# A graph layer on one core: the last steps in another order, and gathers without added waits on VectorE

## The chip, the cores and the metric

The kernel runs on one core of a Trainium2 chip. The metric is device time in microseconds (us), the median of several executions. TensorE (PE) multiplies matrices, and PEld is its loading of weights; VectorE (DVE) and ScalarE (ACT) work on elements; GpSimd (POOL) issues the indirect transfers (gathers) here; SyncE (SP) issues the plain ones, ACT a few of them.

## The reference

One message-passing layer, with residual and normalization. There are 12500 nodes with 128 features (`x`), and 400000 edges with source, destination (sorted) and length (`edge_weight`). What is computed, shortened:

```python
rbf = exp(-(d[:, None] - centers) ** 2 / (2 * width * width))      # 50 centers, 0 to 10
cut = 0.5 * (cos(pi * d / 10) + 1) * (d <= 10)
W = (silu(rbf @ fw1 + fb1) @ fw2 + fb2) * cut[:, None]
messages = (h[src] @ pw + pb) * W
agg = segment_sum(messages, dst)
y = x + (h + silu(agg @ mw1 + mb1) @ mw2 + mb2)                    # h is x
out = (y - mean(y)) / sqrt(var(y) + 1e-5)
```

Edges longer than 10 have `cut` 0 and give nothing.

## The kernel before, in words

Edges of length over 10 are dropped on the chip: in seven chunks (`pack`, `unpack`, L704 to L981) the kept edges are packed together, and they come out as 139 **quads** (`NL`) of 4 times 128 edges. `proj`, which is x times `pw` plus `pb`, is stored in HBM at the start; the first 12 quads gather rows of x and multiply them on the core.

The main loop (L1574) takes one quad `q` per step:

- `fetch` (L1082) gathers 128 rows per instruction (L1088), four to a quad, into one of 21 buffers (`quad`, `x`; 9 from quad 63 on); quads in `SINGLY`, 133 and 134 among them, have only three gathers and get their other rows by single transfers from SP or ACT. How far ahead gathers are put into POOL's queue is set by a planned clock (`clock`, `pool`) and by free buffers (`room`). For quads under `UPTO` (90) each gather has an added wait (L1091 to L1094): on the VectorE instruction that stands a number of places before it in program order, 66 to 19 by `BACK`.
- `basis(o)` (L1129): on ACT, square and exponential of the distances for two quads at once (L1140, L1144); `first(o)` (L1151) and `silu(o)` (L1159) make the hidden layer for them, on PE and ACT. `octs(q)` gives the pair `o` of a step, so that `basis`, `first` and `silu` come two steps or more ahead.
- `second(q + 2)` (L1167) multiplies by `fw2` on PE into a bank of PSUM. There are four such banks; they go round in one list (`bank`, `free`) with all other users.
- `message(q)` (L1178): one product on DVE, bank times gathered rows (L1189), which waits for the last gather of the quad. It gives the bank back.
- `place(q + 1)` (L1196): four instructions on DVE make the 128-wide one-hot tile `hot` (L1201), with `cut` in it. `sum_up(q)` (L1213) multiplies it with the messages on PE (L1221); `add(q)` (L1251) adds the sums into `aggT` on DVE (L1255).
- Nodes go in blocks `t0` of four tiles of 128 nodes, of two tiles from 88 on, as soon as their sums are complete: `node_first` (L1260: PE, then a silu on ACT, `zs`, L1270, which gives the bank back), `node_second` (L1274, PE), `node_stats` (L1299: DVE, L1305 and L1309), and for a group of blocks `variances`, `roots` and `scales` (L1311 to L1340: DVE, a square root on ACT at L1325, DVE). `normalize` (L1342) scales by tiles, on ACT (L1356) or DVE (L1353), and `store` issues the block's transfer to HBM. Blocks 0 to 76 (`early`) have their steps from `begin` (L1392 to L1401); their statistics come in groups of four blocks. 76 has its statistics in step 131.

Every engine works through its instructions in the order of the program; the text above is that order (`manual_schedule`). The last seven steps, quads 132 to 138, are written out one after the other (L1647 to L1753), with the blocks 76 to 96 between them. `house(q)` (L1627) does in them what the loop does for gathers. `keep_busy(n)` (L1435) issues n matmuls whose results nobody reads. The table of ACT's functions is reloaded (ACT_TABLE_LOAD) between square root, exponential and silu. In the step of quad 138 its four products are taken one by one, in `message(q, (0, 1))` and so on.

## Time and profile before

| | |
|---|---|
| runs shown, median of 3 | 720.64 us (720.64 to 723.32) |
| the profiled execution's own time | 718.53 us |
| its span, first to last instruction | 717.0 us |
| mean granted TensorE clock | 0.918 of full |
| DMA | 91.41 MB, mean 127 GB/s |

A profile row of an engine or line gives busy time and count; a row of the timeline gives start and duration in us from the start of the span, engine, line, operation, the program's names (out<-in), shapes, count, and in brackets the engine's idle time just before it and what ended that. Durations are of this one execution, so sums are made against its 718.53 us.

### The profile page before, as it was taken

What the parts mean: (1) busy time and instruction counts of PE and PEld (TensorE: products, weight loads), DVE (VectorE), ACT (ScalarE), POOL (GpSimd) and SP (SyncE); (2) the same over time, 40 slices, a digit from 0 to 9 for tenths busy, and PEclk for the clock granted to TensorE, in tenths of its full rate; (3) what the DMA queues carried; (4) which work ended last, traced back from release to release, by engine and by line L of the source; (5) the groups of instructions that cost most, each with busy time, mean ns of one, the idle gap of its engine ahead of it and who ended that gap; (6) DMA issues with size and microseconds to landing.
All of it is one profiled execution on the core that took longest, in us unless ns stands there. A gap on an engine that the chain in (4) does not pass through costs nothing.

```text
span 717.0 us, 14503 instructions
## 1 busy us (share of the span) xinstructions
PE 584.6 (82%) x3526; PEld 461.1 (64%) x3526; DVE 561.7 (78%) x1741; ACT 401.7 (56%) x569; POOL 529.2 (74%) x565
## 2 busy tenths in 40 slices
PE   5878868688898788697878997799998887878775
PEld 5767557566676576575666765577686654665554
DVE  8899899759998799989979994876856545555765
ACT  6557625245645667554645566466765843574564
POOL 6777777777777777777777777777777777777771
PEclk9998787899999899889987999699999998999997
DMA  8996533333334333443344334444543444344242
GB/s 259 328 328 206 161 99 102 98 102 84 115 103 130 83 87 100 118 126 85 87 113 118 99 116 116 130 131 120 153 113 91 138 111 114 101 142 126 56 131 79
DMA packets 54004, 91.41 MB, mean 127 GB/s; under 512 B 14272, under 2 KB 21536, under 8 KB 53914
## 3 DMA queue, kind: packets, MB, share of 16 engines
q0 software_dynamic: 17712, 36.51, 20.4%
q1 hardware_dynamic: 24916, 35.61, 15.0%
q10 hardware_dynamic: 11286, 18.31, 8.0%
q8 instruction: 29, 0.48, 0.3%
q14 instruction: 61, 0.50, 0.2%
HBM read 74.59 MB, written 15.79 MB: 126 GB/s over the span
## 4 chain that ended last, share of the span: by engine, by line
POOL 18%; DVE 15%; DMA 13%; issue 13%; PE 9%; ACT 3%; ACTq 3%; DVEq 1%; SPq 0%; POOLq 0%
POOL quad L1088 14%; DMA quad<-proj,srci 8%; POOL x L1088 3%; DVE hot L1201 3%; PE ph L1156 3%; DMA x<-proj,srci 3%; DVE msg L1189 2%; ACTq L1064 2%; PE sums L1221 2%; PE bank L1174 1%; DVE aggT L1255 1%; DMA packed<-line,at_i 1%; DVE quad L1189 1%; DMA pair<-packed 1%; DVE quad L1201 1%
## 5 line engine op out<-in xcount | busy, mean ns | idle before, releaser
L1088 POOL DMA_INDIRECT quad<-proj,srci x402 | 381.7, 950 | 122.6 <-issue 97.3
L1174 PEld LDWEIGHTS bank<-fw_sb,s 128*128 128x128 f32 x1112 | 158.1, 205 | 60.3 <-issue 50.2
L1174 PE MATMUL bank<-fw_sb,s 128*128 128x128 f32 x1112 | 158.2, 289 | 0.0
L1156 PE MATMUL ph<-rbf,w_sb 102*128 102x512 f32 x278 | 143.7, 642 | 12.3 <-ACT s L1162 8.3
L1221 PEld LDWEIGHTS sums<-hot,msg 128*128 128x128 f32 x816 | 109.2, 200 | 53.4 <-issue 26.0
L1162 ACT ACTIVATE s<-ph 128x1024 f32<-128x1024 f32 x70 | 71.2, 1017 | 122.3 <-PE ph L1156 121.9
L1201 DVE TENSOR_SCALAR hot<-iota_n,dl,cut 128x80 f32<-128x80 f32 (+4 forms) x408 | 111.1, 347 | 22.9 <-PE sums L1221 20.9
L1221 PE MATMUL sums<-hot,msg 128*128 128x80 f32 (+4 forms) x816 | 111.5, 282 | 15.4 <-DVE msg L1189 15.2
L1088 POOL DMA_INDIRECT x<-proj,srci x94 | 90.0, 958 | 28.7 <-issue 22.3
L1171 PE MATMUL bank<-fb_b,ones_b 96*128 96x512 bf16 x139 | 56.0, 403 | 42.2 <-DVE msg L1189 22.0
L1189 DVE TENSOR_TENSOR msg<-bank,quad 128x512 f32<-128x512 f32 (+1 forms) x78 | 52.5, 673 | 41.1 <-DMA quad<-proj,srci 34.5
L1156 PEld LDWEIGHTS ph<-rbf,w_sb 102*128 102x128 f32 x278 | 51.2, 205 | 51.7 <-issue 37.3
L1255 DVE TENSOR_TENSOR aggT<-aggT,sums 128x80 f32 (+4 forms) x209 | 54.1, 259 | 30.7 <-PE sums L1221 12.4
L1140 ACT ACTIVATE rbf<-d_sb,rbf_bias,rbf_scale 102x512 f32<-102x512 f32 x70 | 56.2, 803 | 8.0 <-issue 8.0
L1088 POOL DMA_INDIRECT quad<-in_x_dram,srci x48 | 47.5, 990 | 15.9 <-issue 12.5
L1162 ACT ACT_TABLE_LOAD x34 | 43.6, 1283 | 15.3 <-issue 14.9
L1144 ACT ACT_TABLE_LOAD x35 | 44.9, 1283 | 11.4 <-issue 9.6
L1221 PE MATMUL sums<-quad,quad 128*128 128x128 f32 (+3 forms) x296 | 41.8, 285 | 11.0 <-DVE quad L1189 11.0
L350 PEld LDWEIGHTS bank<-pw_sb,xT 128*128 128x128 f32 (+1 forms) x292 | 42.3, 209 | 11.2 <-issue 5.6
L1144 ACT ACTIVATE rbf<-rbf 102x512 f32<-102x512 f32 x70 | 44.1, 630 | 7.9 <-issue 5.6
L1221 PEld LDWEIGHTS sums<-quad,quad 128*128 128x128 f32 x296 | 38.6, 201 | 12.7 <-DVE quad L1189 12.4
L350 PE MATMUL bank<-pw_sb,xT 128*128 128x128 f32 (+1 forms) x292 | 42.8, 293 | 0.8 <-ACT xT L995 0.6
(281 smaller groups left out, 796.9 us busy)
## 6 DMA issues: line engine op xcount, KB each, us to landing
d_sb<-near_d ACTq DMA_DIRECT2D x67, 256.0 KB
row_sb<-proj SPq DMA_DIRECT2D x1024, 0.5 KB
x<-in_x_dram SPq DMA_DIRECT2D x46, 256.0 KB
row_sb<-proj ACTq DMA_DIRECT2D x512, 0.5 KB
quad<-proj,srci POOLq DMA_INDIRECT x402
proj<-hp SPq DMA_DIRECT2D x24, 256.0 KB
out_dram<-x SPq DMA_DIRECT2D x22, 256.0 KB
x<-proj,srci POOLq DMA_INDIRECT x94
```

Source lines behind the costliest of these rows:

```text
L350: nc.tensor.matmul(to[:m, k, :], lT[:, k * P:k * P + m], w, start=False, stop=(k == a + c - 1))
L1088: g = nc.gpsimd.indirect_dma_start(out=got[:, j, :], out_offset=None, in_=proj if table is None else table, in_offset=bass.IndirectOffsetO ...
L1140: a = nc.scalar.activation(rbf[:u], d[:u], AF.Square, bias=rbf_bias[:u], scale=rbf_scale[:u])
L1144: nc.scalar.activation(rbf[:u], rbf[:u], AF.Exp, scale=-1.0 / (2.0 * width * width))
L1156: nc.tensor.matmul(ph[:, h, :], w1_sb[:2 * KR, h, :], rbf[:2 * KR], start=True, stop=True)
L1162: nc.scalar.activation(s[:, :n], ph[:, :n], AF.Silu)
L1171: nc.tensor.matmul(pu, ones_b[:, :P], bias_b["fb2"].rearrange("k j f -> k (j f)"), start=True, stop=False)
L1174: nc.tensor.matmul(pu[:, j * H:(j + 1) * H], s[:, j * P:(j + 1) * P], fw2_sb, start=False, stop=(j == QT - 1))
L1189: nc.vector.tensor_mul(msg[:, a:b, :], pu_of[q].rearrange("p (j f) -> p j f", j=QT)[:, a:b, :], got_of[q][:, a:b, :])
L1201: nc.vector.tensor_scalar(hot[:, j, :wide(q)], iota_n[:, :wide(q)], dl[:, at[0], at[1]], cut[:, at[0], at[1]], op0=OP.is_equal, op1=OP.mult)
L1221: nc.tensor.matmul(pa[:, k * W:k * W + wide(q)], msg[:, j, :], hot[:, j, :wide(q)], start=(j % n == 0), stop=(j % n == n - 1))
L1255: nc.vector.tensor_add(to, to, pa[:, k * W:k * W + wide(q)])
```

## The change

Two things are changed.

*Gathers.* `BACK`, `UPTO`, `VECTORS`, the record of VectorE instructions and `behind` go, and with them the added wait in `fetch`. The waits that follow from the data (buffers free, indices there) stay.

*The last steps.*

- The bases of pairs 68 and 69, issued in step 131 so far, are issued in step 132 behind `place(133)`; `first` and `silu` of 68 and 69 go from steps 132 and 133 to 133 and 134.
- In the last steps `second(q + 2)` stands between `message(q)` and `sum_up(q)`, where it stood behind both.
- Block 76 leaves the last group of four: 64, 68 and 72 have their root in step 129 and are normalized in 130 to 132; 76 has its statistics at the end of step 130 and is in one group with 80, 84, 88 and 90.
- `node_stats` of 80 to 92 stand ahead of `add` or earlier; 76 and 80 are normalized together in step 136; block 88 is normalized on DVE; `node_x(96)` stands ahead of the sums of 136.
- `keep_busy` is called with 3, 2 and 2 in place of 1 and 1.

```diff
-            g = nc.gpsimd.indirect_dma_start(
+            nc.gpsimd.indirect_dma_start(
                 out=got[:, j, :], out_offset=None, in_=proj if table is None else table,
                 in_offset=bass.IndirectOffsetOnAxis(ap=i, axis=0))
-            if 0 <= q < UPTO and len(vectors) > behind(q):
-                tc.add_manual_dep(
-                    g.ins, vectors[-1 - behind(q)],
-                    mybir.DependencyInfo(mybir.DependencyClass.Sync, mybir.DependencyReason.DATA))
...
-            if begin[t0][2] == q:
+            if begin[t0][2] == q and t0 != early[-1]:
                 if k % 4 == 0:
                     st_of[0] = statistics()
                 node_stats(t0, st_of[0][:, k % 4 * 4:])
-                if k % 4 == 3:
+                if k % 4 == 3 or t0 == early[-2]:
                     deep.append(deviations(early[k // 4 * 4:k + 1], st_of[0]))
...
     def tail(q):
 
+        if q == NL - 9:
+            last_st.append(statistics())
+            node_stats(early[-1], last_st[0])
...
-                if 2 * o < NL:
+                if 2 * o < NL and q < NL - 8:
                     basis(o)
...
     q = NL - 7
     house(q)
-    sum_up(q, message(q))
+    msg = message(q)
     second(q + 2)
+    sum_up(q, msg)
+    node_second(84)
+    node_stats(80, last_st[:, 4:])
     bases_of(list(range(q, NL)))
     place(q + 1)
-    scales(*deep.pop(0))
+    for o in (octs(q), octs(q + 1)):
+        basis(o)
     add(q)
-    first(octs(q))
-    silu(octs(q))
-    node_second(84)
     normal(1)
-    st = statistics()
-    node_stats(80, st)
 
     q += 1
     house(q)
-    sum_up(q, message(q))
+    msg = message(q)
     second(q + 2)
-    first(octs(q))
-    silu(octs(q))
-    normal(1)
+    first(octs(q - 1))
+    silu(octs(q - 1))
+    sum_up(q, msg)
     place(q + 1)
+    node_stats(84, last_st[:, 8:])
     add(q)
     node_first(88)
-    node_stats(84, st[:, 4:])
     load_x(92)
 
     q += 1
     house(q)
-    sum_up(q, message(q))
+    msg = message(q)
     second(q + 2)
+    first(octs(q - 1))
+    silu(octs(q - 1))
+    sum_up(q, msg)
     node_second(88)
     place(q + 1)
     add(q)
-    normal(1)
     node_first(90)
-    node_stats(88, st[:, 8:])
+    node_stats(88, last_st[:, 12:])
     load_x(94)
-    normal(1)
 
     q += 1
     house(q)
-    sum_up(q, message(q))
+    msg = message(q)
     second(q + 2)
     node_second(90)
+    sum_up(q, msg)
     place(q + 1)
+    node_stats(90, last_st[:, 14:])
+    dev = deviations([76, 80, 84, 88, 90], last_st)
+    silu_next()
     add(q)
     load_x(96)
-    node_stats(90, st[:, 10:])
-    dev = deviations([80, 84, 88, 90], st)
-    silu_next()
 
     q += 1
     house(q)
-    sum_up(q, message(q))
+    msg = message(q)
     second(q + 2)
+    node_x(96)
+    sum_up(q, msg)
     place(q + 1)
-    node_x(96)
     st = statistics()
+    scales(*dev)
     add(q)
     node_first(92)
-    scales(*dev)
-    normal(1)
+    normal(2)
     place(q + 2)
 
     p, q = NL - 2, NL - 1
     house(p)
-    sum_up(p, message(p))
+    msg = message(p)
     node_second(92)
+    keep_busy(3)
+    sum_up(p, msg)
+    node_stats(92, st)
     sum_up(q, message(q, (0, 1)), (0,))
     add(p)
     node_first(94)
+    sum_up(q, message(q, (1, 2)), (1,))
     normal(1)
-    sum_up(q, message(q, (1, 2)), (1,))
-    node_stats(92, st)
     add(q, (0,))
+    keep_busy(2)
     sum_up(q, message(q, (2, 3)), (2,))
-    normal(2)
+    normalize(*ready.pop(0), on=(0, 1))
+    store()
+    normal(1)
     node_second(94)
-    keep_busy(1)
     sum_up(q, message(q, (3, 4)), (3,))
     add(q, (1,))
     node_first(96)
     node_stats(94, st[:, 2:])
+    keep_busy(2)
     dev = variances([92, 94], st)
-    keep_busy(1)
     nc.scalar.activation(warm, half_pi, AF.Sqrt)
```

More of the change, by code (lines that the diff above doesn't have):

```diff
@@ L60 @@
 LISTS = 5
-BACK = ((0, 66), (16, 38), (26, 46), (39, 38), (52, 26), (63, 19), (88, 46), (102, 14),
-        (111, 8))
-UPTO = 90
-VECTORS = ("TensorScalarPtr", "TensorTensor", "CopyPredicated", "TensorReduce", "TensorCopy",
-           "BNStats")
 SPILL = 4
@@ L440, in before_it @@
         return max((m for m in range(q) if place_of(m) == place_of(q)), default=-1)
-    vectors = []
-    def logged(i):
-        if i.engine == mybir.EngineType.DVE and str(i.opcode) in VECTORS:
-            vectors.append(i.name)
-    nc.push_inst_callback(logged)
-    def behind(q):
-        return next(n for at, n in reversed(BACK) if q >= at)
     def room(q):
@@ L1425, in nodes @@
                 load_x(t0)
-    st_of, deep = {}, []
+    st_of, deep, last_st = {}, [], []
     def tail(q):
+        if q == NL - 9:
+            last_st.append(statistics())
+            node_stats(early[-1], last_st[0])
         for k, t0, step in ((9, 80, node_first), (8, 80, node_second), (8, 84, node_first)):
@@ L1645, in normal @@
             store()
-    assert not todo and counted and not ready and len(deep) == 1 and done[0] == NL - 7
+    assert not todo and counted and not ready[1:] and not deep and done[0] == NL - 7
+    last_st = last_st[0]
     q = NL - 7
     house(q)
-    sum_up(q, message(q))
+    msg = message(q)
     second(q + 2)
+    sum_up(q, msg)
+    node_second(84)
+    node_stats(80, last_st[:, 4:])
     bases_of(list(range(q, NL)))
     place(q + 1)
-    scales(*deep.pop(0))
+    for o in (octs(q), octs(q + 1)):
+        basis(o)
     add(q)
-    first(octs(q))
-    silu(octs(q))
-    node_second(84)
     normal(1)
-    st = statistics()
-    node_stats(80, st)
     q += 1
     house(q)
-    sum_up(q, message(q))
+    msg = message(q)
     second(q + 2)
-    first(octs(q))
-    silu(octs(q))
-    normal(1)
+    first(octs(q - 1))
+    silu(octs(q - 1))
+    sum_up(q, msg)
     place(q + 1)
+    node_stats(84, last_st[:, 8:])
     add(q)
     node_first(88)
-    node_stats(84, st[:, 4:])
     load_x(92)
@@ L1753 @@
     store()
-    nc.remove_inst_callback(logged)
     def more(q):
```

## The prediction, made before the changed kernel had run

> **What bounds the kernel now.** I read the page's busy times first, then the waits of POOL (total, count, longest), then the view of the gathers' line L1088 (min/median/max).

> ```profile
> PE 584.6 (82%) x3526; PEld 461.1 (64%) x3526; DVE 561.7 (78%) x1741; ACT 401.7 (56%) x569; POOL 529.2 (74%) x565
> ```
> ```profile
> POOL quad L1088 <- issue: 109.8, 360, 0.3
> ...
> POOL quad L1088 <- DVE aggT L1255: 2.4, 8, 0.3
> ...
> POOL quad L1088 <- DVE srci L566: 1.6, 1, 1.6
> ```
> ```profile
> L1088 POOL DMA_INDIRECT quad<-proj,srci x402: 940/944/1192, 72.2 to 700.4; - x134
> L1088 POOLq EVENT_SEMAPHORE x165: 17/17/749, 11.8 to 689.3; - x165
> ...
> L1088 POOL DMA_INDIRECT quad<-in_x_dram,srci x48: 940/944/1300, 6.8 to 70.9; - x48
> ```

> No engine is full by its share of the span, yet POOL never rests: idle time ahead of a gather is 0.3 us, whatever ended it, and only the first one waited longer (1.6). So 0.94 of work and 0.3 of issue make a period of 1.25 us from 6.8 to 700.4. POOL sets when the last gather is issued; the end is that plus what is left behind it. How much is left, the timeline of the end shows, after one row of the chain of waits for the time from issue to landing:

> ```profile
> 667.90 2.50 DMA quad<-proj,srci
> ```
> ```profile
> 675.50 0.69 DVE L1189 TENSOR_TENSOR msg<-bank,quad 128x512 f32<-128x512 f32 x1 [0.22 <-DMA quad<-proj,srci]
> ...
> 685.44 0.94 POOL L1088 DMA_INDIRECT quad<-proj,srci  x1 [0.30 <-issue]
> ...
> 692.12 0.69 DVE L1189 TENSOR_TENSOR quad<-bank,quad 128x512 f32<-128x512 f32 x1
> ...
> 700.42 0.94 POOL L1088 DMA_INDIRECT quad<-proj,srci  x1 [0.30 <-issue]
> ...
> 706.29 0.48 DVE L1189 TENSOR_TENSOR quad<-bank,quad 128x128 f32<-128x128 f32 x2
> ```

> Quad 132's product (675.50) still waits for its gather. Quad 135's last gather, issued at 685.44, lands at 687.9; its product starts at 692.12, 4.2 late. The last gather of all, quad 138's, lands at 702.9; its product is the second of the two at 706.29, so at 706.5, **3.6 us late**, and the end (717.0) is 10.5 after that. So the gathers bound the kernel up to 675, and a backlog of some 4 us that arises between 675 and 687 bounds its end. Where it arises:

> ```profile
> 670.53 0.69 DVE L1189 TENSOR_TENSOR quad<-bank,quad 128x512 f32<-128x512 f32 x1 [0.85 <-DMA quad<-proj,srci]
> 670.89 0.60 ACT L1270 ACTIVATE zs<-bank 128x512 f32<-128x512 f32 x1 [5.03 <-PE bank L1268]
> 671.14 0.68 DVE L1305 SCALAR_TENSOR_TENSOR x<-x,bank 128x512 f32<-128x512 f32 x1
> 671.51 1.28 ACT L1325 ACT_TABLE_LOAD   x1
> ...
> 671.85 0.87 DVE L1309 BATCH_NORM_STATS2 st<-x 128x6 f32<-128x128 f32 x4
> ...
> 673.65 0.80 ACT L1140 ACTIVATE rbf<-d_sb,rbf_bias,rbf_scale 102x512 f32<-102x512 f32 x1
> ...
> 675.34 1.12 PE L1268 MATMUL bank<-aggT,mw_sb 128*128 128x512 f32 x2 [0.30 <-DVE aggT L1255]
> ...
> 677.78 1.28 ACT L1270 ACT_TABLE_LOAD   x1
> ...
> 679.07 0.60 ACT L1270 ACTIVATE zs<-bank 128x512 f32<-128x512 f32 x1
> 679.72 0.38 PE L1171 MATMUL bank<-fb_b,ones_b 96*128 96x512 bf16 x1 [2.32 <-ACT zs L1270]
> ...
> 680.83 1.88 PE L1156 MATMUL ph<-rbf,w_sb 102*128 102x512 f32 x4
> ...
> 682.55 0.38 PE L347 MATMUL bank<-mb_b,ones_b 96*128 96x512 bf16 x1
> ...
> 683.66 1.06 PE L1221 MATMUL sums<-hot,msg 128*128 128x128 f32 x8
> 683.67 1.63 ACT L1356 ACTIVATE x<-x,by,rs 128x128 f32<-128x128 f32 x4
> ...
> 684.55 0.38 PE L1171 MATMUL bank<-fb_b,ones_b 96*128 96x512 bf16 x1
> ...
> 684.75 0.61 DVE L1255 TENSOR_TENSOR aggT<-aggT,sums 128x128 f32 x2 [2.47 <-PE sums L1221]
> ```

> The product of `node_first(84)` ends at 676.5 on PE, but its silu starts only at 679.07: ACT has the root of the group's deviations and both last bases in front of it (671.5 to 677.8), and then a table load (677.78). The silu holds the bank that `second(134)` needs, and PE stands 2.32 us. Then PE runs without a rest, with the sums of quad 133 only at 683.66, behind `second`, `first` and `node_second`; the add waits 2.47 for them, and the next products, behind that add in DVE's queue, move with it.

> **The change part by part.** *The gathers' waits.* Gathers of quads under 90 lose a wait each. One stretch with these waits and one behind quad 90 without them, from the gathers' line by windows (POOL busy and count come first):

> ```profile
> 400.00:440.00 40.00, 30.38 (x32) 1.00 0.38 115
> 560.00:600.00 40.00, 30.26 (x32) 0.96 0.46 128
> ```

> That is 949 and 946 ns each, and 32 in 40 us both times. A wait instruction takes 17 ns and lies within the 0.3 us. From one side: 165 of them, all on the path, would be 2.8 us to gain. From the other: gathers that met as much beside them as the slowest of the first 48 would take up to 1300 instead of 944. I take 0, as the nearest row, 0.3 idle with and without, has it. Nothing else becomes late: the waits for data stay, and none ended after the 0.3.

> *Block 76 and the roots.* Block 76's statistics (0.68 and 0.87 on DVE) go from step 131 to 130, where DVE waits for a gather anyway (0.85 at 670.53); the group of four becomes three and its root is taken in step 129; two normalizations (1.63 of ACT each) go from the tail to steps 130 and 131, where ACT idles (5.03 at 670.89). In step 131 ACT then has neither root nor bases ahead of the silu of 84: it starts at 676.5, 2.5 earlier, and PE's 2.32 goes.

> *The two last bases* cost the same 4.1 us of ACT (673.65 to 677.8), a step on; by the code they issue no transfer any more, since the distances and single rows have all been asked for. What is late next: ACT runs this silu to 677.1, the bases to 681.2, a normalization to 682.8, a table load of 1.28 and `silu(68)` of 1.0, to 685.1. `second(136)` in step 134 needs it. PE's starts above give 1.11 for `second` (679.72 to 680.83), 1.72 for `first`, 1.11 for `node_second`, 0.89 for sums. With `second(136)` at 685.2, a one-quad `first(69)` (0.86) and sums (0.89), the sums of 134 end at 688.1, the add at 688.7, block 88's statistics at 689.6, and quad 135's product is 1.7 late, not 4.2. Then PE needs 2.6 us (135: `second`, half a `node_second`, sums) and 3.4 us (136, with `node_x`) of the 5.0 that four gathers take, so the backlog is gone in 136.

> *`second` ahead of the sums, statistics ahead of adds.* PE no longer stands for a product before work that doesn't need it; no instruction is added. On SP, the stores of 64 and 68 leave earlier; x of 96 waits for the store of 72 (normalized by 682.8), well ahead of `node_x`.

> *The end*, from two windows of all engines and the timeline:

> ```profile
> 692.12:695.54 3.42, 2.67 (x22) 2.58 (x22) 2.39 (x7) 2.66 (x5) 2.51 (x4) 1.00 0.68 211
> 695.54:698.95 3.41, 1.02 (x9) 0.87 (x8) 3.08 (x12) 1.59 (x2) 2.72 (x3) 1.00 0.36 92
> 698.95:702.37 3.42, 3.42 (x17) 3.21 (x16) 2.97 (x12) 0.20 (x1) 1.88 (x2) 0.50 0.23 56
> ```
> ```profile
> 698.09 1.31 PE L1221 MATMUL sums<-hot,msg 128*128 128x128 f32 x8 [2.39 <-DVE msg L1189]
> ...
> 703.57 0.38 ACT L1270 ACTIVATE zs<-bank 128x256 f32<-128x256 f32 x1 [4.41 <-PE bank L1268]
> ...
> 706.95 0.27 PE L347 MATMUL bank<-mb_b,ones_b 96*128 96x256 bf16 x1
> ...
> 707.51 0.38 PE L1439 MATMUL ph<-mb_b,ones_b 96*128 96x512 bf16 x1
> ...
> 707.73 0.38 PE L1221 MATMUL sums<-quad,quad 128*128 128x128 f32 x2
> ```

> Normalizations of 76 and 80 (3.3 us of ACT) stand between the silus of 92 and 94, instead of 80's alone; 88's goes to DVE, 0.6. With the silu of 92 at some 698 against 703.57, ACT is free by 701.7 and this is hidden behind the gathers; without that cover it costs 1.6. Five more filler matmuls of 0.22 (707.51 to 707.73) are 1.1 us in PE's waits for products. PE was busy 1.02 of the 3.41 us up to 698.95, and the granted clock after it is 0.50: that too comes of the backlog, since PE stood 2.39 for a product.

> [...]

> Last, quad 138's last sums stand at 707.73 behind `node_second(94)` (706.95) and a filler, 0.9 after their product (706.8). If the products come at 703.0, `node_second(94)` fits between two of them: 0.6 less.

> **The sum** against the profiled execution (718.53: span 717.0 and 1.5 around it): waits 0; last product 3.5 earlier (706.5 to 703.0, as soon as its gather is there); 0.6 behind it: **-4.1 us**, span 712.9, 714.4 in its own time. The median of the runs shown, 720.64, is 2.1 above the profiled one; off that, **716.5**. The last gather's landing does not move, so the gain can't be much larger.

> **The rivals.** *Half the gain.* PE's window from 695.5 has by these steps the sums of 136, `node_first`, `node_second(92)` and three fillers: some 1.7 us of 3.4, between the 1.02 that halved the clock and the 2.67 that didn't. If the clock halves from 699 to 702, some 1 to 2 us of PE's work between the last products come on top: 717.5 to 718.5. For it: the window is thin; against it: the fillers lie exactly there.

> *No gain.* ACT's chain to `silu(68)` has no slack. If it is 2 us longer, step 135 starts as late as now, and with a halved clock the last product is near 706.5 again: 720.6. Against it: the 5.0 us of a step leave PE 1.6 to 2.4 to catch up.

> *Slower: gathers against VectorE.* Without the waits the 300 gathers of quads 12 to 90 could run beside other VectorE work and take longer. Place: POOL, where all of it is on the path. Price: at 30 ns each 9 us, 725.5; it outweighs the tail's gain from 14 ns a gather. For it: there are gathers of 1192 and 1300 ns. Against it: as no wait ended late, no start moves, and the median is 944 in every group.

> [...]

> **How the numbers follow.** Tail catches up (715.0 to 717.5): 0.58. Half the gain: 0.23. No gain: 0.10. Slower by the gathers: 0.05; by a clock that is halved over more of the tail, or by something unseen: 0.04. Half a percent, 3.6 us, is about what a measurement of this kernel can tell from no change; its bound, 717.04, lies inside the first case, so 0.04 of that go to "within". Faster 0.54, within 0.5% 0.37, slower 0.09. The range goes from 713.8 (runs of one kernel lie up to 2.7 apart, 720.64 to 723.32) to 720.6, the end of "no gain".

> **What would show it.** Right: gathers still 0.3 apart, the last issued near 700.4; no wait of PE for the silu near 677; quad 135's product under 2 late, quad 138's right behind its landing; less than 10 us from there to the end. Wrong: gathers of 960 on average (third rival), `second(136)` waiting for ACT past 687 (second), clock 0.50 after 699 (first). A new wait of the tail that starts after 690, where no slack of a step is left to make up for it, would make the prediction wrong.

## The result and the profile after

| | before | after |
|---|---|---|
| median | 721.4 us, 6 runs (720.64 to 723.32) | 716.65 us, 6 runs (715.16 to 718.23) |
| profiled execution, its span | 718.53, 717.0 | 715.16, 713.5 |
| last gather issued | 700.42 | 699.40 |
| from there to the end of the span | 16.6 | 14.1 |

The ratio is 0.9934, 95% interval [0.9916, 0.9952]: faster by 4.75 us, or 3.5 to 6.1 by the interval. The prediction was 716.5. Ratios and intervals, here and below, leave out executions over 1.5% above the fastest of the same kernel, so they need not be the ratios of the medians shown.

First the waits of POOL after (total, count, longest), then the view of the gathers' line, now L1070 (min/median/max of one, first and last start, count):

```profile
POOL quad L1070 <- issue: 104.6, 343, 0.3
...
POOL quad L1070 <- DVE srci L548: 1.6, 1, 1.6
```
```profile
L1070 POOL DMA_INDIRECT quad<-proj,srci x402: 940/944/1185, 71.5 to 699.4; - x134
L1070 POOLq EVENT_SEMAPHORE  x159: 17/17/1088, 12.2 to 688.1; - x159
```

A gather still takes 944 ns, and POOL's idle time ahead of one is still 0.3 us. Only 6 of its 165 wait instructions are gone, so most of the waits taken out had no instruction of their own. Then the timeline of after where the backlog arose before:

```profile
673.52 1.02 PE L1246 MATMUL bank<-aggT,mw_sb 128*128 128x512 f32 x2
674.58 0.60 ACT L1248 ACTIVATE zs<-bank 128x512 f32<-128x512 f32 x1 [2.26 <-PE bank L1246]
...
675.07 0.80 ACT L1118 ACTIVATE rbf<-d_sb,rbf_bias,rbf_scale 102x512 f32<-102x512 f32 x1
675.23 0.38 PE L1149 MATMUL bank<-fb_b,ones_b 96*128 96x512 bf16 x1 [0.68 <-ACT zs L1248]
...
682.04 1.02 ACT L1140 ACTIVATE s<-ph 128x1024 f32<-128x1024 f32 x1
...
684.42 0.95 POOL L1070 DMA_INDIRECT quad<-proj,srci  x1 [0.30 <-issue]
...
688.32 0.69 DVE L1167 TENSOR_TENSOR quad<-bank,quad 128x512 f32<-128x512 f32 x1
```

The roles have changed: ACT now waits for PE's product of block 84 (2.26), not PE for ACT (0.68, where it was 2.32). The bases follow at 675.07, `silu(68)` is through at 683.06 (682.04 and 1.02). Quad 135's last gather, issued at 684.42, lands 2.5 later (2.50 in the prediction's row), at 686.9; its product is 1.4 late, not 4.2. Now the end, from the timeline and, for the last gather, the chain of waits:

```profile
697.04 0.69 DVE L1167 TENSOR_TENSOR msg<-bank,quad 128x512 f32<-128x512 f32 x1 [0.82 <-DMA quad<-proj,srci]
...
697.93 12.11 SPq L188 DMA_DIRECT2D out_dram<-x  x7
...
699.40 0.94 POOL L1070 DMA_INDIRECT quad<-proj,srci  x1 [0.30 <-DMA quad<-proj,srci]
...
701.59 0.61 PE L345 MATMUL bank<-mw_sb,zs 128*128 128x128 f32 x4
703.63 0.29 DVE L1167 TENSOR_TENSOR quad<-bank,quad 128x128 f32<-128x128 f32 x1 [2.03 <-DMA quad<-proj,srci]
703.98 0.49 PE L1199 MATMUL sums<-quad,quad 128*128 128x128 f32 x2 [1.79 <-DVE quad L1167]
...
706.08 1.06 PE L1273 MATMUL bank<-mw_sb,zs 128*84 128x128 f32 x4
```
```profile
699.40 4.21 DMA quad<-proj,srci
```

Quad 137's product waits for its gather again (0.82), so the backlog is gone. The last product (703.63) starts 0.02 after its gather has landed, and `node_second(94)` (701.59) is done by then, both as predicted. What is new is the 4.21 us from the last gather's issue to its landing. Before it was 2.54 (700.42 to 702.97 in the trace).

### The profile page after: what moved, and what is told of

The parts are those of the page before. It is cut to its first block, busy times and chain, and to the rows that moved or that the text cites. A ratio compares the mean times of both kernels' runs of the same rounds, so it can differ in the third digit from the quotient of the medians.

```text
span 713.5 us, 14510 instructions
## 1 busy us (share of the span) xinstructions
PE 588.6 (82%) x3531; PEld 462.0 (65%) x3531; DVE 561.9 (79%) x1743; ACT 402.6 (56%) x568; POOL 528.1 (74%) x565
## 4 chain that ended last, share of the span: by engine, by line
DVE 27%; PE 19%; DMA 16%; POOL 16%; issue 12%; ACT 4%; ACTq 3%; DVEq 2%; SPq 0%; POOLq 0%
DMA quad<-proj,srci 11%; POOL quad L1070 9%; POOL x L1070 6%; PE ph L1134 6%; DVE hot L1179 4%; PE bank L1152 4%; PE sums L1199 3%; DVE msg L1167 3%; ACTq L1046 2%; DVE aggT L1233 2%; DVE quad L1179 2%; DMA x<-proj,srci 2%; DVE r_d L511 2%; PE bank L345 2%; DVE nodes L521 1%
## 5 line engine op out<-in xcount | busy, mean ns | idle before, releaser
L1070 POOL DMA_INDIRECT quad<-proj,srci x402 | 381.4, 949 | 122.7 <-issue 92.8
L1134 PE MATMUL ph<-rbf,w_sb 102*128 102x512 f32 x278 | 145.5, 649 | 11.1 <-ACT s L1140 7.1
L1140 ACT ACTIVATE s<-ph 128x1024 f32<-128x1024 f32 x70 | 71.2, 1017 | 116.6 <-PE ph L1134 116.3
L1070 POOL DMA_INDIRECT x<-proj,srci x94 | 89.9, 956 | 28.7 <-issue 24.4
L1070 POOL DMA_INDIRECT quad<-in_x_dram,srci x48 | 47.0, 979 | 15.9 <-issue 11.9
L1199 PEld LDWEIGHTS sums<-quad,quad 128*128 128x128 f32 x296 | 39.4, 205 | 12.1 <-DVE quad L1167 11.4
```

The lines of the kernel that those rows point to most:

```text
L1070: nc.gpsimd.indirect_dma_start(out=got[:, j, :], out_offset=None, in_=proj if table is None else table, in_offset=bass.IndirectOffsetOnAxi ...
L1134: nc.tensor.matmul(ph[:, h, :], w1_sb[:2 * KR, h, :], rbf[:2 * KR], start=True, stop=True)
L1140: nc.scalar.activation(s[:, :n], ph[:, :n], AF.Silu)
L1199: nc.tensor.matmul(pa[:, k * W:k * W + wide(q)], msg[:, j, :], hot[:, j, :wide(q)], start=(j % n == 0), stop=(j % n == n - 1))
```

## The experiments

My theory: the gain is the tail's, by ACT's queue in front of the silu of 84, and the waits are worth nothing. The rivals: the waits are worth the 1.0 us by which POOL ended earlier; the order of the products or the fillers carry the gain. The late landing needed a cause too. Unless said otherwise, "issue to end" is the time from the last gather's issue to the end of the span in the kernel's profile.

Of the four groups of experiments, each measured together on one chip with the kernel before, two ran where that kernel takes about 720 us, as in the pair above; they are the first four experiments and the two on stores. The other six, told together at the end, ran on two chips where the same kernel takes 1.5 times as long, and say little of the tail. Each experiment has one profile, so what is read from a profile is one execution.

### Only the waits taken out

```diff
-            g = nc.gpsimd.indirect_dma_start(
+            nc.gpsimd.indirect_dma_start(
...
-            if 0 <= q < UPTO and len(vectors) > behind(q):
-                tc.add_manual_dep(
```

> The kernel before with the gathers' added waits taken out and nothing else changed. Theory: every such wait had been satisfied long before its gather's turn, so POOL still issues a gather each 1.25 us, the last one within 0.2 us of 700.4, and the time is that of before (721.4; 720.5 to 722.3). First rival: the waits cost POOL something; in the changed kernel the last gather was issued at 699.40, 1.02 earlier, and if that is the waits' doing the time here is 720.4 and the last gather is issued near 699.4. Second rival: without them the gathers meet more VectorE work and take longer than 946 ns on average: slower than 722.5.

Measured: 720.26, before 720.03, ratio 1.0005 [0.9987, 1.0022]. Its waits of POOL and its gathers' line:

```profile
POOL quad L1088 <- DVE at_row L937: 3.0, 1, 3.0
```
```profile
L1088 POOL DMA_INDIRECT quad<-proj,srci x402: 939/945/1192, 71.6 to 703.3; - x134
```

Median duration 945 ns, against 944 with the waits: the second rival falls. The last gather was expected within 0.2 of 700.42; it left late (703.29) because of a single wait of 3.0 us, for a VectorE instruction of a chunk's packing (`at_row`), so for data, since no other waits are left. Where the kernel before takes 720, the last gather leaves at 700.22 to 700.50 in the four profiles with the added waits, and at 699.40, 699.89, 700.34 and 703.29 in the four without. So 1.02 between two profiles is no price of the waits. A wait for `at_row` of over 0.3 us stands in two of the four without them (3.0, and 0.5 with the bases back) and in none of the four with them; whether the added waits keep it off is not shown. By issue to end this kernel is like before: 719.6 - 703.29 = 16.3.

### Only the tail

The diff is the change's without its part in `fetch`: `BACK`, `UPTO`, `behind` and the added wait stay.

> The changed kernel with the gathers' added waits put back, so only the last steps differ from before. Theory: the whole gain is the last steps', so 716.7 (715.8 to 717.6), PE's wait for the silu of block 84 near 675 under 1 us and the last gather's product at its landing. Rival: the missing waits bring 1.0 us (the last gather's issue at 699.40 instead of 700.42): then 717.7 with the last gather issued near 700.4.

Measured: 717.07, ratio 0.9963 [0.9948, 0.9977], PE's wait for the silu of 84 0.69, last gather issued at 700.22. The time is the theory's; POOL's end is where the rival had it, but it doesn't set the time alone, since here the last gather landed late too. PE's wait from the timeline, then the landing from the chain of waits:

```profile
675.93 0.38 PE L1171 MATMUL bank<-fb_b,ones_b 96*128 96x512 bf16 x1 [0.69 <-ACT zs L1270]
```
```profile
700.22 4.42 DMA quad<-proj,srci
```

The second measurement of the same kernel (below) gave 0.9945 [0.9925, 0.9965]. These intervals overlap that of the whole change (the first only from 0.9948 to 0.9952); with the run before this one, nothing of the gain is left for the waits that these runs could show. By the interval of that run, 0.9987 to 1.0022, a gain of up to 0.9 us or a loss of up to 1.6 would not be seen.

### The bases back in step 131

```diff
-                if 2 * o < NL and q < NL - 8:
+                if 2 * o < NL:
...
-    for o in (octs(q), octs(q + 1)):
-        basis(o)
```

> The changed kernel with the two last bases in step 131 again (4.1 us of ACT ahead of the silu of block 84); first and silu of the pairs stay in steps 133 and 134. Theory: the silu of 84 waits for ACT again; ACT stood 2.26 us ahead of it, so it starts some 1.9 later, near 676.5, PE waits some 2 us for the bank, quad 133's product is about 2 late, and of that the four steps to 136 make good all but some 0.5: 716.7 to 717.7. Rival: the backlog is not made good, as in the kernel before, and with it comes a thin PE window and half a clock before the last products: 719 to 721. Second rival: the bases' place is worth nothing at all, and what counts is the order of the products ahead of the sums: 716.7 with PE's wait near 675 under 1 us.

Measured: 718.86, ratio 0.9986 [0.9967, 1.0006], that is 1.8 slower than the tail alone, measured beside it. (The tail alone has the added waits, this kernel doesn't. Against the kernel without fillers, below, which lacks them too, it is 2.5 slower.) From its timeline:

```profile
676.05 1.02 PE L1246 MATMUL bank<-aggT,mw_sb 128*128 128x512 f32 x2
...
678.22 0.63 ACT L1122 ACTIVATE rbf<-rbf 102x512 f32<-102x512 f32 x1
...
678.87 1.28 ACT L1248 ACT_TABLE_LOAD   x1
680.16 0.60 ACT L1248 ACTIVATE zs<-bank 128x512 f32<-128x512 f32 x1
...
680.81 0.38 PE L1149 MATMUL bank<-fb_b,ones_b 96*128 96x512 bf16 x1 [3.74 <-ACT zs L1248]
...
693.76 0.69 DVE L1167 TENSOR_TENSOR quad<-bank,quad 128x512 f32<-128x512 f32 x1
...
700.34 0.95 POOL L1070 DMA_INDIRECT quad<-proj,srci  x1 [0.30 <-issue]
...
706.74 0.28 DVE L1167 TENSOR_TENSOR quad<-bank,quad 128x128 f32<-128x128 f32 x1
```

PE's product of 84 ends at 677.07, but ACT has the bases and a table load in front of its silu (680.16), and PE stands 3.74. Quad 135's product is at 693.76; its last gather left at 685.28 and landed at 687.89 in the trace: 5.9 late. The last product (706.74) comes 3.9 after its gather's landing (702.86 in the trace). The backlog is there again, and only 2.0 of the 5.9 is made good by the end: my theory ("all but some 0.5") was wrong. The first rival was right that the backlog stays, wrong on the clock (full from 665.28 to 713.06 in this profile), and its 719 to 721 was just missed. This one place in ACT's queue makes the difference between a last product at once and one 3.9 late. That shows the bases' move to be needed; that it is enough by itself is not shown, since the kernel with nothing else changed ran only on a slower chip (below).

Only 1.8 of that shows in the time. In this kernel the last gather lands in 2.5 us; in the tail alone it needs 4.4 and its product comes at 704.66. So 706.74 - 704.66 = 2.1 is what was won. The median with the bases back is still 1.2 under the 720.03 of before, which the bases don't explain; its interval reaches 1, and by issue to end (16.45 against 16.57) its profile shows nothing of it.

### Without the fillers ahead of the last products

```diff
-    keep_busy(3)
...
-    keep_busy(2)
     sum_up(q, message(q, (2, 3)), (2,))
```

> The changed kernel without the three filler matmuls ahead of the sums of quad 137 and the two ahead of the third sums of quad 138 (the last two stay). Theory: the fillers hold PE's share of the windows from 695 to 702 over a half; without them one of these windows has about 1.5 of 3.4 us of work, the granted clock is 0.50 for at least 3.4 us between 697 and 705, and PE's work there takes some 1.5 us longer. The last gather lands only at 703.6, so part of that is hidden: 717 to 718.5. Rival: fillers change nothing, since a halved clock is hidden behind the last landing and the stretch from 705.4 has half a clock in any case: 716.7 within 0.5, perhaps 0.3 less as 1.1 us of fillers go.

Measured: 716.38, ratio 0.9954 [0.9939, 0.9969], beside 0.9963 for the tail alone (which has the added waits): no difference, and the rival's time. Its windows of all engines (PE's busy time first, the granted clock third from the end), cut where the clock changed:

```profile
694.65:698.06 3.41, 1.71 (x10) 0.93 (x8) 2.50 (x11) 1.58 (x5) 2.56 (x3) 1.00 0.22 56
698.06:701.47 3.41, 3.10 (x12) 2.62 (x13) 1.97 (x8) 1.88 (x5) 2.17 (x3) 0.50 0.54 186
701.47:704.89 3.42, 2.84 (x11) 2.30 (x11) 1.20 (x5) 2.49 (x7) 0.00 (x0) 0.50 0.12 31
704.89:708.30 3.41, 3.21 (x12) 1.99 (x11) 1.76 (x9) 1.33 (x3) 0.00 (x0) 0.50 0.43 154
```

The mechanism came as expected: PE was busy 1.71 of 3.41 us, and the clock was half for the next 10.2. The expected price does not show in the time, but it does in the profile:

```profile
703.69 0.28 DVE L1167 TENSOR_TENSOR quad<-bank,quad 128x128 f32<-128x128 f32 x1
```

The last product was 1.0 behind its landing (703.69 against 702.73), and from the landing to the end it took 12.1 us, against 9.9 to 10.8 in the four profiles with the fillers and the bases moved. It was hidden because in this execution the last gather landed 2.84 after its issue, not 4.15 to 4.42. Whether it did so in the other executions is not on record. So what the fillers are worth in the time stays open; it is below what these runs tell apart, some 1.5 us.

### Are the stores what delays the last gather?

The tail alone was measured once more, and beside it the same kernel with the stores of 76 to 90 bound to the product behind the last gather:

```diff
-            eng.dma_start(d, s) if store else eng.dma_start(s, d)
+            i = eng.dma_start(d, s) if store else eng.dma_start(s, d)
+            if late and store:
+                tc.add_manual_dep(i.ins, late[0].name, ...)
...
-    sum_up(q, message(q, (3, 4)), (3,))
+    msg = message(q, (3, 4))
+    late.append(product[0].ins)
+    store()
+    late.clear()
+    sum_up(q, msg, (3,))
```

> The changed kernel with the gathers' added waits put back, once more. On a chip where the kernel before takes 720 to 722: as measured before, ratio 0.995 to 0.998 (717.1), the last gather landing over 4 us after its issue (4.42 in its first profile). On a chip as in the last two calls, where the kernel before takes 1067 to 1069 and the changed one 1.7% more: if the missing waits are what costs there (the bases-only kernel, which has the waits, was at 1.0016), the ratio is 0.995 to 1.005; if the last steps are, it is 1.012 to 1.022.

> The kernel beside it, with the stores of blocks 76, 80, 84, 88 and 90 held back until the product behind the last gather. Theory, where the kernel before takes 720 to 722: the last gather lands 2.5 to 2.6 after its issue, not 4.4, and the time is 1.0 to 1.8 less than the kernel beside it: ratio 0.993 to 0.995. Rival: the late landing has another cause, and the two times agree within 0.5. Second rival: the landing comes earlier, but the held stores run into the last ones, and the end is the same or later. On a chip as in the last two calls, the last gather lands long before these stores in any case, and the two kernels differ by no more than their intervals.

Measured: the tail alone 715.92, ratio 0.9945 [0.9925, 0.9965], just under the 0.995 expected; with the stores held 715.43, ratio 0.9947 [0.9925, 0.9969]. From their chains of waits, the tail alone first, then with held stores:

```profile
700.34 4.15 DMA quad<-proj,srci
```
```profile
700.50 3.33 DMA quad<-proj,srci
```

And the stores in the timeline of the second:

```profile
703.85 0.29 DVE L1197 TENSOR_TENSOR quad<-bank,quad 128x128 f32<-128x128 f32 x1 [1.09 <-DMA quad<-proj,srci]
...
704.22 2.41 SPq L195 DMA_DIRECT2D out_dram<-x  x5
```

With no store in flight the landing took 3.33, 0.8 less but not 2.5, and the time is the same. Over all profiles where the kernel before takes 720: with these stores in flight 4.21, 4.42, 4.15 and 2.84; without 2.54, 2.58, 2.53 and 3.33. The two groups overlap: the stores are not the whole cause, and of my expectations for the held stores the rival's was right for the time and neither for the landing. Holding them gives no version that is measurably better.

What else is in flight, the DMA packets in the traces tell. The last gather's rows come as 16 packets of 4 KB. In some executions a packet of 16 KB, of the kind that the page's list of DMA queues calls `instruction`, falls among them. Times in us from the gather's issue:

| profile | `instruction` packet | last of the 16 starts | landing |
|---|---|---|---|
| before | none before 7.24 | 2.04 | 2.54 |
| only the waits out | none before 7.32 | 2.00 | 2.58 |
| bases back | none before 5.72 | 2.03 | 2.53 |
| without fillers | 2.50 to 3.42 | 2.27 | 2.84 |
| tail alone, stores held | 1.30 to 2.22 | 2.20 | 3.33 |
| tail alone, second | 2.11 to 3.03 | 3.02 | 4.15 |
| changed | 2.02 to 2.94 | 3.15 | 4.21 |
| tail alone, first | 1.99 to 3.13 | 3.35 | 4.42 |

In the last four, one of the 16 packets starts only about when that packet is through, and all others are through by 2.6; where it lies behind them or is absent, none is late. With stores in flight the 16 start some 0.3 later (from 1.94 to 2.01, against 1.65 or 1.66). So the landing goes with the `instruction` packet in all eight profiles and, by a few tenths, with the stores. No run moved that packet alone, so this is read from the order of the packets and not tested. Its place went with PE's in these two: it came around `node_second(94)` (701.59 in the changed kernel, 706.95 in before), at 701.42 and 707.66. When the backlog went, this transfer too came earlier, and met the last gather.

### On chips where the kernel before takes 1067 to 1069 us

Four kernels ran on one such chip and two on another: the changed one twice, held stores on the changed one twice, and

```diff
 y2: steps 132 to 136 of the changed kernel
-    second(q + 2)
     sum_up(q, msg)
+    second(q + 2)
 y4: the kernel before
-                if 2 * o < NL:
+                if 2 * o < NL and q < NL - 8:
...
+    for o in (octs(q), octs(q + 1)):
+        basis(o)
```

with `first` and `silu` a step later in y4, as in the change. In the table, y2 is "changed, sums first" and y4 is "before, bases a step later".

> The changed kernel once more, unaltered, beside the three that follow, so that they have it on the same chip. Measured before: 716.65 (715.16 to 718.23), ratio 0.9934 [0.9916, 0.9952]. Expected: 716 to 717.2, ratio 0.993 to 0.996. What is to be seen in its profile: whether the last gather again lands over 4 us after its issue (4.2 in its first profile, 4.4 with the waits put back, 2.8 without fillers), and when POOL issues it (699.40 in the first profile; 699.9 to 703.3 in others).

> The changed kernel with the stores of blocks 76, 80, 84, 88 and 90 held back until the product behind the last gather (a wait of their queue on that product; the normalizations stay where they are). Theory: these stores, in flight from 698 on, lengthen the last gather's way from issue to landing from 2.5 to 4.2 us; without them it is 2.5 to 2.6 again, the last product is 1.6 earlier and the time some 1.5 less than the changed kernel's on this chip: 714.6 to 715.7. Rival: the late landing has another cause (the gather's own rows), it stays over 4 us, and the time is the changed kernel's within 0.5. Second rival: the landing is 1.6 earlier but the held stores (some 1 MB, over 5 us at the 180 GB/s of 698 to 702) run into the last stores: same or up to 2 us slower.

> The changed kernel with the sums of quads 132 to 136 ahead of second (and of first, node_second and node_x) again, as before; all else as changed. Theory: PE then stands for the product of each quad, 0.7 to 1 us a step, but the steps have 1.6 to 2.4 us to spare, so quads 135 and 136 are up to 1 later and the end 0 to 0.5: 716.6 to 717.2. Rival: the order is what brings the 1.2 us that the bases' place (718.9 with the bases back, 720.0 before) leaves unexplained: 717.6 to 718.5. Second rival: sums first free the adds and products sooner, and the time is 0.5 less.

> The kernel before with one thing changed: the bases of pairs 68 and 69 in step 132 behind the place of 133, first and silu of them in steps 133 and 134. Theory: ACT has only the root and its two table loads ahead of the silu of 84, PE's wait for it is under 1 us, not 2.3, and most of the backlog is gone: 717.3 to 718.5, that is two thirds of the gain. Rival: the bases only move the stall (the root and 76's normalizations still crowd ACT, silu of pair 68 late in step 133): 719.5 to 721. Second rival: they are all of it: 716 to 717.

> The changed kernel, unaltered, beside the next one, since the last four kernels ran on a chip where the kernel before took 1069 us. Expected where the kernel before takes 720 to 722: ratio 0.993 to 0.996, so 716 to 717.5; the last gather lands 2.8 to 4.4 after its issue. Expected on a chip as the last one: ratio 1.008 to 1.026 as there.

> The changed kernel with the stores of blocks 76, 80, 84, 88 and 90 held back until the product behind the last gather. Theory: the last gather lands 2.5 to 2.6 after its issue, not 2.8 to 4.4, and the time is 0.8 to 1.6 less than the changed kernel's of the same call: ratio to before 0.991 to 0.994. Rival: the late landing has another cause, it stays at 2.8 to 4.4 and the times agree within 0.5. Second rival: the landing comes earlier, but the held stores run into the last ones and the end is the same or later.

| kernel | median | ratio, interval |
|---|---|---|
| changed (first chip) | 1081.04 | 1.017 [1.008, 1.026] |
| changed, stores held | 1078.34 | 1.015 [1.0065, 1.0236] |
| changed, sums first | 1081.08 | 1.0162 [1.0077, 1.0247] |
| before, bases a step later | 1068.45 | 1.0016 [0.9955, 1.0076] |
| changed (second chip) | 1084.11 | 1.0174 [1.0136, 1.0212] |
| changed, stores held | 1084.04 | 1.0187 [1.0146, 1.0228] |

The second measurement of the changed kernel repeats the first, as expected of it on such a chip. The times and ratios expected of the first four did not come; their theories of the tail, made for 720, could be neither met nor missed here, so what the order of `second` and the sums, and the bases alone, are worth is untested. A stretch of the changed kernel's timeline shows what is different:

```profile
614.65 0.37 PE L1152 MATMUL bank<-fw_sb,s 128*128 128x128 f32 x1 [1.81 <-issue]
...
617.44 0.35 PE L1199 MATMUL sums<-quad,quad 128*128 128x112 f32 x1 [2.43 <-issue]
...
619.56 0.35 PE L1199 MATMUL sums<-quad,quad 128*128 128x112 f32 x1 [1.77 <-issue]
```

In stretches like this one, TensorE lets matmuls go some 2 us apart, with nothing that the profile shows to wait for; the mean clock of the six profiles is 0.76 to 0.78. POOL no longer sets the pace: it waits for products, up to 19.3 us at a time, where at 720 no gather but the first and two behind `at_row` waited over 0.3. From the waits of POOL in the changed kernel:

```profile
POOL quad L1070 <- DVE msg L1167: 120.6, 22, 19.3
```

In that condition the change as a whole is 1.7% slower by the ratios and 1.1 and 1.6% by the medians (before: 1069.29 and 1067.18), and the loss is not in the tail. Windows of 200 us, first of the changed kernel, then of before with late bases, which has the waits (PE's matmuls in the first bracket):

```profile
300.00:500.00 200.00, 115.77 (x558) 89.79 (x557) 95.79 (x275) 61.74 (x75) 106.42 (x112) 0.70 0.23 64
500.00:700.00 200.00, 137.05 (x737) 105.44 (x736) 134.30 (x386) 78.53 (x96) 87.93 (x92) 0.81 0.25 72
```
```profile
300.00:500.00 200.00, 135.92 (x691) 106.79 (x692) 124.38 (x349) 81.55 (x97) 95.22 (x100) 0.77 0.24 69
500.00:700.00 200.00, 128.95 (x642) 99.26 (x640) 114.26 (x335) 64.51 (x79) 105.95 (x111) 0.76 0.25 70
```

From 300 to 500 it is 558 matmuls against 691, in a stretch where the two programs differ in nothing but the gathers' waits; from 500 to 700 most of that is caught up, but not all. Counted from the start, all five profiles without the waits have 1406 to 1413 matmuls by 500 and 3178 to 3214 by 1000; the one with them has 1574 and 3264. By 500 POOL is ahead without them (275 instructions against 268) while PE is behind. The last gather leaves at 1027.0 in the one and 1013.4 in the other, and at 1022 to 1035 in all five profiles without the waits; from there to the end they need 51.5 and 55.2. So what was lost was lost ahead of the tail. Only one kernel with the waits was profiled there, the tail alone was not run there, and how the waits help is not shown. That they matter where POOL doesn't set the pace is what these runs point to.

## Why the prediction was right, step by step

**What bounds.** Right: gathers 0.3 apart to the end, in after and in every profile at 720, but for the two waits for `at_row` (3.0 and 0.5). Not foreseen: the place of the last gather, which the prediction held fixed at 700.42, lies at 699.40 to 700.50 in seven of the eight profiles and at 703.29 in one.

**The waits at 0.** Right within what the runs tell apart, where the kernel takes 720 (1.0005 with only them gone). The rival of gathers against VectorE is excluded there: 945 ns without, 944 with the waits. That VectorE's work lengthens a gather at all, and the 30 ns of the rival's price, were the author's supposition; no run shows them. Where POOL did not set the pace, on the slower chips, the waits seem to count, which the prediction didn't consider.

**Block 76, the roots and the bases.** Right in place and sign: 2.32 became 0.68. The prediction had the silu of 84 at 676.5 and `silu(68)` done at 685.1; they came at 674.58 and 683.06, both 2 earlier, since PE's product was itself less late (it ended at 674.54, in before at 676.46). Quad 135 was predicted 1.7 late and was 1.4; in before it was 4.0 late, not the 4.2 of the prediction, as its gather took 2.69. That the gain needs the bases' move is shown by putting them back: 3.9 late at the last product, about as in before (3.5 by the landing in the trace, 3.6 in the prediction). That experiment also corrects the argument against the rival "no gain", that a step leaves PE 1.6 to 2.4 to catch up: from quad 135 to the last product, over three steps, only 2.0 of 5.9 was made good.

**`second` ahead of the sums.** Not tested where the tail matters; its own part is not shown, nor that of block 76's move.

**The end.** The term for the last product was mis-sized in one piece, and the sentence "the last gather's landing does not move" was wrong. Predicted 703.0, as soon as its gather is there; measured 703.63, as soon as its gather was there, but the gather needed 4.21 us instead of 2.5, while POOL was 1.02 earlier. From the last gather's issue, the tail gained 16.6 - 14.1 = 2.5, not 4.1 (with stores held 16.6 - 13.4 = 3.2). The 0.6 behind the last product came as 10.5 to 9.9. In the medians the sum was -4.75 in the first pair, and -3.0 and -3.8 for the tail alone in its two measurements (717.07 against 720.03, 715.92 against 719.75), around the predicted 4.1. That 716.5 met 716.65 so closely is luck in part: in the profile a landing 1.7 too slow and a POOL 1.0 too early nearly cancel, and the median of before was 721.4 in that measurement, not the 720.64 that the forecast started from.

**The clock.** The rival "half the gain" had the right mechanism in the wrong place. The window that it put at 1.7 us of work had 2.83 (695.15 to 698.56 in after); without five of the fillers it had 1.71. The clock stayed full from 699 to 702 and was halved from 705.39. From the windows of after, then of the tail alone in its second measurement:

```profile
698.56:701.98 3.42, 3.05 (x20) 2.13 (x18) 1.99 (x9) 2.42 (x8) 1.48 (x2) 1.00 0.62 211
701.98:705.39 3.41, 1.34 (x8) 0.80 (x8) 1.14 (x5) 1.15 (x3) 0.00 (x0) 1.00 0.45 156
705.39:708.80 3.41, 1.75 (x7) 0.90 (x5) 2.41 (x17) 2.48 (x6) 0.00 (x0) 0.50 0.03 7
```
```profile
700.95:704.36 3.41, 2.06 (x13) 1.33 (x11) 1.00 (x4) 2.69 (x7) 0.34 (x1) 1.00 0.39 127
704.36:707.77 3.41, 2.31 (x11) 1.28 (x11) 2.26 (x11) 1.30 (x2) 0.00 (x0) 1.00 0.38 134
```

The tail is the same instructions in both. PE's wait for the last product, 1.79 in the one and 1.70 in the other, fell into one window in after (1.34 busy, half a clock behind it) and was cut by a border in the other (2.06, full). The half clock made the four products of block 96 (L1273) 1.06 instead of 0.67, but that late it cost little: from landing to end 9.9 and 10.8 where it came behind the last landing (after, and the tail alone the first time, from 704.83), 10.0 and 10.1 where it stayed full (the tail alone the second time, and with stores held). Where it came at 698.06, without five fillers, that stretch took 12.1: the rival's price of 1 to 2 us is there, though an early landing hid it in that profile and the medians don't show it. Without the five fillers the clock halved behind a window of 1.71 us of work in which PE had no rest over 0.81.

## What to carry to other kernels

Read the last stage from its end: see which product is late behind its transfer, follow the lateness back to the first wait of an engine that should have been ahead, and look at what stands in front of that instruction in the releaser's queue; here 4.1 us of work that nobody needed yet decided between 0 and 3.9 us at the last product. When a backlog goes, the transfers that it had delayed start earlier (here a 16 KB `instruction` packet at 701.42 instead of 707.66), so allow the last transfer more than its usual duration (here 2.8 to 4.4 us in place of 2.5) and look at what its packets meet. A median without a difference doesn't show that two effects are absent: read the profile for a second one that hides the first. A gain of half a percent has to be placed by profiles and by pairs measured together, and it can turn round on a chip where another engine sets the pace.

## What the runs showed of the hardware that was not expected

```profile
695.75 0.70 PE L1246 MATMUL bank<-aggT,mw_sb 128*128 128x256 f32 x2 [0.81 <-DVE aggT L1233]
696.92 0.27 PE L342 MATMUL bank<-mb_b,ones_b 96*128 96x256 bf16 x1 [0.47 <-ACT zs L1248]
...
698.30 0.58 PE L1199 MATMUL sums<-hot,msg 128*128 128x128 f32 x1 [0.67 <-DVE msg L1167]
```

  None is over 0.81 us: here several short rests in one window left it with 1.71 us of work, and the clock behind it was half.
- Two of the chips ran the kernel before at 1067 to 1069 us instead of 720. In the profiles there (of the changed kernel and its variants) stretches have matmuls about 2 us apart, and the mean clock is 0.76 to 0.78; on them the changed kernel was 1.017 times before.
- A gather's landing went with a 16 KB `instruction` packet (0.92 to 1.14 us each here): 3.33 to 4.42 us where it lay among the gather's packets, 2.53 to 2.84 where it did not.
